# Layer norms of a hybrid convolution and attention kernel applied as one broadcast factor a token, with a second buffer for copied attention and an earlier norm of the next band

## The chip, the cores and the metric

The kernel runs on 1 core of one Trainium2 chip. The metric is the device time of one execution in microseconds (us). The kernel before took 956.23 us in the median of 9 runs (953.95 to 963.8).

## The reference, cut to what matters

The input x has 4 images of 128 channels on 64 x 64 pixels. Two layers follow each other.

```python
# layer 0: windowed attention
y = layernorm over channels (eps 1e-6) * g + b
y = y + depthwise 3x3 convolution(y)
# 16x16 windows, 2 branches, 4 heads of 32; each pixel attends to its 5x5 neighbours in the window
x = x + (ho[:, 0] + 0.5 * ho[:, 1]) / sqrt(1.25)

# layer 1: tokens t = pixels, 128 channels
t = t + linear_attention(ln(t), W, b)      # q, k = elu(.) + 1; causal sums over all earlier tokens
t = t + recurrence(ln(t), W, V)            # batch norm of ln(t) @ W.T, then y = sigmoid(wx + y @ V.T)

def ln(v, eps=1e-5):                       # over the 128 channels of a token
    return (v - mean(v)) / sqrt(var(v) + eps)
```

Both norms of layer 1 feed a matrix product over the channels. So (v - mean) @ W is v @ (C W) with C = I - 1/128, and the factor 1/sqrt(var + eps) of a token may be applied to the product's result as well as to its input.

## The kernel before, in words

The work is cut into 16 bands (4 images, 4 bands of 16 pixel rows each), a band into 4 windows of 16 x 16 pixels, and for layer 1 into 2 halves of 512 tokens. The order of the work is written by hand: one loop over 64 windows ("places") emits the instructions, and at its end `in_order` pins each of TensorE (PE), VectorE (DVE), ScalarE (ACT) and GpSimd (POOL) to the order of emission. The DMAs stand on SyncE's queue (SP) in the order of the framework's own scheduling. Every matmul result goes through one pool of 8 PSUM banks (`bank`, L172), taken in turn.

At place i three windows are in work, in this order:

- `logits` of window i (L362, L367), with exponentials on ACT (L376).
- `scaled` of window i - 2 on POOL (L425): the copied attention `o_sb` times the broadcast reciprocals `rden`, into `oT`.
- `weighted` of window i - 1: row sums (L385), their copy `den` (L388) and its DMA to `dc` (L390); weighted sums of values (L397) and their copy on ACT to `o_sb` (L405); reciprocals on DVE (L408 to L412), a DMA of them to DRAM (L414) and one from DRAM to all partitions, `rden` (L416). Both `o_sb` and `rden` have one buffer.
- `window_inputs` of window i + 1: queries, keys and values (L322 to L345).

Between these parts there are 6 numbered gaps a place (`between`, L678). In each gap two generators move on by one step:

- `behind` is layer 1 of the band before, `layer1` (L594), a written list of 24 steps of which 24 gaps of four places take one each, beginning at the second place of a band, gap 0. Its operations: `output0` (L450, L457: output projection and residual), `measure` (mean and variance by bn_stats on DVE, then 1/sqrt on POOL by L195, L196), `norm` (four DVE instructions of L203), `turn` (four PE transposes by L212, copied to SBUF by ACT, L474), `queries`, `keys`, `values` (L479 to L504), `scores`, `accumulate`, `attend`, and then, for the second norm, `measure` again, `norm`, `keep` (transposes of the un-normed tokens, an ACT copy, a DMA to DRAM), `turn_last` (transposes of the normed tokens, an ACT copy, L582) and `product` (L587, an ACT copy to `wx`, L588, statistics on DVE, L589).
- `ahead` is `front` (L648): layer norm of the next band (`norm_rows`, L212 with input `xf`) and its convolution (`convolve`, L271 and L273). In the first place of a band it moves only in gaps 0, 4 and 5. `norm_rows` measures group g, scales group g - 1 and turns group g - 2 in one step, so that a group's transposes come in the step after its scaling.

After the last place `run(behind)` and `layer1_end` finish layer 1 of the last band with nothing beside them. Then 8 MB of kept tokens come back by four DMAs (`res`, L733, two each on the SP and the ACT queue), and the recurrence runs: 11 warming steps and 32 steps of two groups (L756 to L808).

The lines that set the emission order of a gap:

```python
    def between(i, gap):
        next(behind, None)
        if i < len(places) and (i == 0 or i % NB or gap in (0, 4, 5)):
            next(ahead, None)
```

Of the kernel before, what the change touches and what calls it, by code (L numbers as in the profile page):

```python
# [46 lines left out]
def conv_attn_hybrid(ctx: ExitStack, tc: tile.TileContext, ins: dict, out: bass.AP):  # L47
# [10 lines left out]
    def loaded(name, shape, dt=F32, src=None, eng=None):  # L58
# [19 lines left out]
        pattern=[[1, P]],  # L78
        channel_multiplier=-1,
    )  # L80
    mhalf = const.tile([P, NCH], F32, name="mhalf")
    nc.vector.memset(mhalf, -0.5)

# [49 lines left out]
    def prepare():  # L133


        rect = math.sqrt(1.0 + LAM * LAM * (BR - 1))
        nc.vector.tensor_scalar(woT[:, 0], woT[:, 0], 1.0 / rect, None, ALU.mult)
        nc.vector.tensor_scalar(woT[:, 1], woT[:, 1], LAM / rect, None, ALU.mult)
        nc.vector.tensor_scalar(ab1, ab[:, :2], 1.0, None, ALU.add)


    dmax = const.tile([P, 16], F32, name="dmax")
# [56 lines left out]
    def normed(found, tiles, tag):  # L199
        pieces, mv, rs = found  # L200
        xn = tiles.tile([P, 4, P], F32, tag=tag, name=tag)
        for j, piece in enumerate(pieces):
            nc.vector.tensor_scalar(  # L203
                xn[:, j, :], piece, mv[:, j, 0:1], rs[:, j : j + 1], ALU.subtract, ALU.mult
            )
        return xn
# [17 lines left out]
    def norm_rows(n):  # L224

        b, wi = bands[n]
        y = padded(n)
        below = wi < NB - 1
        first, end = (0 if wi == 0 else 1), NCH + below

        def evict(dst, src):
            nc.scalar.activation(dst, src, AF.Identity, bias=ln_b, scale=ln_g)

        groups = [(0, 4), (4, 8), (8, 9)] if wi == 0 else [(1, 5), (5, end)]

        found, xn = {}, {}
        for g in range(len(groups) + 2):
            if g < len(groups):
                found[g] = measured(
                    [xin[n][:, j, :] if j < NCH else heads.pop(n + 1) for j in range(*groups[g])],  # L240
                    1e-6,
                )
            if g - 1 in found:
                xn[g - 1] = normed(found.pop(g - 1), p2, "xf")
            if g - 2 in xn:
                j0, j1 = groups[g - 2]
                rows = turned(xn.pop(g - 2), 0, j1 - j0)[:, : (j1 - j0) * P]
                rows = rows.rearrange("p (r w) -> p r w", w=W)
                k1 = min(2 * j1 + 1, WS + 2)
                evict(y[:, 2 * j0 + 1 : k1, 1 : W + 1], rows[:, : k1 - 2 * j0 - 1, :])  # L250
                if j1 > NCH:
                    evict(padded(n + 1)[:, 1:3, 1 : W + 1], rows[:, 2 * (NCH - j0) :, :])
            yield
        ks = slice(1, WS + 1 + below)
        nc.gpsimd.tensor_copy(y[:, ks, 0:1], y[:, ks, 1:2])
        nc.gpsimd.tensor_copy(y[:, ks, W + 1 :], y[:, ks, W : W + 1])

        if wi == 0:
            nc.gpsimd.tensor_copy(y[:, 0, :], y[:, 1, :])
        if below:  # L260
            nc.gpsimd.tensor_copy(padded(n + 1)[:, 0, :], y[:, WS, :])
        else:
            nc.gpsimd.tensor_copy(y[:, WS + 1, :], y[:, WS, :])
# [115 lines left out]
    def weighted(w):  # L379


        ops, dps = bank(), bank()
        for h in range(HEADS):
            rows = slice(h * HD, (h + 1) * HD)
            nc.tensor.matmul(dps[rows], ones[:, :HD], w["es", h], start=True, stop=True)  # L385

        den = p1.tile([P, BR * WT], F32, tag="den", name="den")
        nc.scalar.copy(den, dps)  # L388
        dc = p2.tile([P, 16], F32, tag="dc", name="dc")
        nc.sync.dma_start(dc, den[::HD, :])  # L390
# [13 lines left out]
        o_sb = p1.tile([P, BR * WT], F32, tag="o_sb", name="o_sb")  # L404
        nc.scalar.copy(o_sb, ops)  # L405
# [12 lines left out]
        yield  # L418
# [45 lines left out]
            del oTs[h.n], xin[h.n]  # L464

    def measure(h):
        h.found = measured([h.x[:, j, :] for j in range(4)], 1e-5)

    def norm(h):
        h.xn = normed(h.found, p3, "xn")  # L470

    def turn(h):
        h.xl = p2.tile([P, 512], F32, tag="xl", name="xl")
        nc.scalar.copy(h.xl, turned(h.xn, 0, 4))  # L474

    def feature(h, m):

# [95 lines left out]

    def keep(h):

        rs = p1.tile([P, SEG, HSEGS], F32, tag="rs_o", name="rs_o")
        nc.scalar.copy(rs, turned(h.x, 0, 4).rearrange("p (k s) -> p s k", s=SEG))
        nc.sync.dma_start(resd[h.b][:, h.hb], rs.rearrange("p s k -> p (s k)"))

    def turn_last(h):  # L580
        h.xl = p2.tile([P, 512], F32, tag="xl2", name="xl2")
        nc.scalar.copy(h.xl, turned(h.xn, 0, 4))  # L582

    def product(h):

        wps = bank()
        nc.tensor.matmul(wps, fwT, h.xl, start=True, stop=True)  # L587
        nc.scalar.copy(wx[:, h.b, h.hb], wps.rearrange("p (k s) -> p s k", s=SEG))  # L588
        nc.vector.bn_stats(  # L589
            stats[:, h.b * NH + h.hb, :], wx[:, h.b, h.hb].rearrange("p s k -> p (s k)")  # L590
        )

    def layer1(n, last):

        a, c = Half(n, 0), Half(n, 1)
        y, z = last
        order = [
            (keep, z), None,
            (norm, z), (product, y), None,
            (output0, a), (measure, a), None,  # L600
            (turn_last, z), None,
            (norm, a), (output0, c), (measure, c), None,
            (turn, a), None,
            (product, z), (norm, c), None,
            (queries, a), None,
            (keys, a), None,
            (turn, c), None,
            (values, a), None,
            (queries, c), None,
            (scores, a), None,  # L610
            (keys, c), None,
            (turn_keys, a), None,
            (values, c), None,
            (accumulate, a), None,
            (turn_keys, c), None,
            (attend, a, 0), None,
            (attend, a, 1), (measure, a), None,
            (scores, c), (keep, a), None,
            (accumulate, c), (norm, a), None,
            (attend, c, 0), None,  # L620
            (turn_last, a), (attend, c, 1), (measure, c), None,
        ]
# [7 lines left out]
    halves = {}  # L630

    def layer1_end(y, z):
        norm(z)
        product(y)
        yield
        keep(z)
        turn_last(z)
        yield
        product(z)

# [5 lines left out]
    def front():  # L646


        for n in range(1, len(bands)):
            yield from norm_rows(n)  # L650
            if bands[n][1]:
                yield
            for half in range(2):
                yield from convolve(n, half)
                yield
            if n == 1:

                for _ in range(4):
                    yield


    nc.vector.tensor_scalar(cpe_w[:, 4:5], cpe_w[:, 4:5], 1.0, None, ALU.add)
# [14 lines left out]
    def between(i, gap):  # L677


        next(behind, None)  # L680
        if i < len(places) and (i == 0 or i % NB or gap in (0, 4, 5)):
            next(ahead, None)

    for i in range(len(places) + 2):
# [5 lines left out]
        if 2 <= i:  # L690
            m, wjm = places[i - 2]
            if wjm == NB - 1:
                run(behind)
                behind = layer1(m, halves.pop(m - 1, (None, None)))
        between(i, 0)
        if 2 <= i:
            scaled(m, wjm, windows.pop(i - 2))
# [802 lines left out]
```

## Time and profile before

| what | value |
|---|---|
| median of 9 runs | 956.23 us |
| the profiled execution's own time | 954.84 us |
| its span, first to last instruction | 952.8 us |
| mean granted TensorE clock | 0.979 |
| PE busy | 877.9 us (92%) |
| DVE busy | 745.5 us (78%) |
| ACT busy | 543.5 us (57%) |
| POOL busy | 262.7 us (28%) |

Span and own time differ by 2.0 us, which lie around the first and the last instruction. A page line such as `L212 PE MATMUL bank<-ident,xn ... x256` is one group: source line, engine, operation, written and read tiles, count. In the views of waits, "A <- B: total, times, longest" says that A's engine was idle before A until B was done. In the view of windows each row is a stretch of time, then the busy time of PE, PEld (weight loads), DVE, ACT and POOL, the granted clock, the share of the 16 DMA engines that was busy and GB/s.

Of the span, about 33 us pass before the second place, the places and their gaps last until about 841 us, the end of layer 1 until 880 us, and the recurrence until 952.8 us.

### The profile page before, as it was taken

Reading aid. Unit: us, or ns where it says so; the run is one execution under the profiler, and the core shown is the slowest. Engines: PE = TensorE matmul, PEld = TensorE weight load, DVE = VectorE, ACT = ScalarE, POOL = GpSimd, SP = SyncE. Lnnn points to the kernel's source line nnn. Section 1 sums busy time; section 2 is a strip of 40 time slices with the busy share of each in tenths; the row PEclk is TensorE's granted clock in tenths of the full one; section 3 lists DMA queues with packets and bytes.
Section 4 is the critical chain, followed back from the end, with each engine's and each line's share of the span. In section 5 each row is a group of like instructions: output and inputs, shape, how many; then the busy total and the mean of one; then the engine's idle time right before and its main releaser. Section 6 shows DMA issues by size and latency. Waiting matters only on the chain.

```text
span 952.8 us, 26560 instructions
## 1 busy us (share of the span) xinstructions
PE 877.9 (92%) x10508; PEld 654.3 (69%) x10508; DVE 745.5 (78%) x2452; ACT 543.5 (57%) x1010; POOL 262.7 (28%) x359
## 2 busy tenths in 40 slices
PE   5979999999999999999999999999999999967784
PEld 3757777777777777677777777786767778645442
DVE  6445979887887878797878879887878787567786
ACT  3555656565756565665657565656666564522553
POOL 2113131413232322413132323223141312131185
PEclk9988999999999999999999999999999999999898
DMA  4111121211212121212112121211121111100853
GB/s 124 28 36 60 48 69 37 55 60 49 58 60 59 49 54 55 61 37 64 51 47 59 58 58 58 51 58 55 48 69 36 55 39 51 40 34 30 352 205 148
DMA packets 53045, 63.46 MB, mean 67 GB/s; under 512 B 22960, under 2 KB 33840, under 8 KB 52400
## 3 DMA queue, kind: packets, MB, share of 16 engines
q1 hardware_dynamic: 51184, 56.91, 19.1%
q10 hardware_dynamic: 1728, 4.77, 1.3%
q8 instruction: 85, 1.39, 0.6%
q14 instruction: 48, 0.39, 0.1%
HBM read 35.44 MB, written 17.30 MB: 55 GB/s over the span
## 4 chain that ended last, share of the span: by engine, by line
PE 69%; DMA 10%; DVE 9%; ACT 5%; POOL 3%; issue 2%; SPq 1%; ACTq 0%; POOLq 0%; DVEq 0%
PE bank L322 9%; PE bank L450 6%; PE bank L367 6%; PE bank L212 6%; DMA rden<-rd 6%; PE bank L397 5%; PE bank L385 5%; PE bank L335 5%; PE bank L479 5%; PE bank L558 3%; PE bank L587 3%; PE bank L539 3%; PE bank L522 3%; PE bank L560 3%; DMA res<-resd 2%
## 5 line engine op out<-in xcount | busy, mean ns | idle before, releaser
L273 DVE SCALAR_TENSOR_TENSOR y<-ypad,cpe_w,y 128x512 f32<-128x512 f32 x240 | 188.7, 786 | 12.9 <-ACT y L271 9.3
L425 POOL TENSOR_TENSOR oT<-o_sb,rden 128x512 f32<-128x512 f32 x64 | 85.3, 1332 | 361.2 <-DMA rden<-rd 335.0
L376 ACT ACTIVATE es<-bank 128x512 f32<-128x512 f32 x256 | 132.2, 602 | 77.2 <-PE bank L367 77.2
L196 POOL TENSOR_TENSOR rs<-rs,mhalf 128x4 f32<-128x4 f32 (+2 forms) x100 | 106.8, 1068 | 8.3
L367 PEld LDWEIGHTS bank<-q,k 32*128 32x128 f32 x3072 | 99.0, 191 | 10.7 <-ACT k L330 9.6
L367 PE MATMUL bank<-q,k 32*128 32x96 f32 (+1 forms) x3072 | 97.6, 273 | 8.7 <-ACT k L330 8.7
L203 DVE TENSOR_SCALAR xn<-x,mv,rs 128x128 f32<-128x128 f32 x256 | 83.3, 386 | 21.5 <-POOL rs L196 21.5
L195 POOL TENSOR_SCALAR rs<-mv 128x4 f32<-128x4 f32 (+2 forms) x100 | 24.9, 249 | 269.6 <-DVE mv L193 181.8
L397 PEld LDWEIGHTS bank<-es,v_sb 128*32 128x32 f32 x3072 | 57.2, 111 | 30.5 <-issue 18.7
L405 ACT COPY o_sb<-bank 128x512 f32<-128x512 f32 x64 | 37.6, 587 | 66.5 <-POOL oT L425 48.3
L479 PE MATMUL bank<-xl,awT 128*128 128x512 f32 x128 | 70.1, 631 | 1.0 <-ACT xl L474 1.0
L385 PE MATMUL bank<-es,ones 128*32 128x512 f32 x512 | 70.8, 626 | 0.0
L397 PE MATMUL bank<-es,v_sb 128*32 128x96 f32 (+1 forms) x3072 | 70.3, 240 | 0.0
L450 PE MATMUL bank<-woT,oT 128*128 128x128 f32 x512 | 65.6, 283 | 4.1 <-POOL oT L425 4.0
L450 PEld LDWEIGHTS bank<-woT,oT 128*128 128x128 f32 x512 | 62.4, 196 | 7.9 <-POOL oT L425 5.1
L322 PE MATMUL bank<-y2w,wqT 128*128 128x256 f32 x256 | 66.3, 382 | 1.4 <-DVE y2w L273 1.4
L342 ACT COPY v_sb<-bank 128x512 f32<-128x512 f32 x64 | 37.6, 588 | 51.3 <-PE bank L335 50.3
L322 PE MATMUL bank<-y2w,wkT 128*128 128x256 f32 x256 | 65.8, 380 | 0.0
L335 PE MATMUL bank<-wvT,y2w 128*128 128x256 f32 x256 | 65.8, 380 | 0.0
L330 ACT COPY q<-bank 128x512 f32<-128x512 f32 x64 | 37.8, 591 | 37.8 <-PE bank L322 37.4
L191 DVE BATCH_NORM_STATS2 st<-x 128x6 f32<-128x128 f32 x256 | 55.5, 279 | 1.1
L212 PE MATMUL bank<-ident,xf 128*128 128x128 f32 x128 | 31.5, 332 | 24.5 <-DVE xf L203 20.4
(124 smaller groups left out, 1741.7 us busy)
## 6 DMA issues: line engine op xcount, KB each, us to landing
rden<-rd SPq DMA_DIRECT2D x64, 256.0 KB
v_sb<-v_sb SPq DMA_DIRECT2D x128, 64.0 KB
resd<-rs_o SPq DMA_DIRECT2D x32, 256.0 KB
out<-ot SPq DMA_DIRECT2D x32, 256.0 KB
xin<-in_xt SPq DMA_DIRECT2D x15, 512.0 KB
res<-resd SPq DMA_DIRECT2D x2, 2048.0 KB
res<-resd ACTq DMA_DIRECT2D x2, 2048.0 KB
dc<-den SPq DMA_DIRECT2D x64, 8.0 KB
```

Source lines behind the costliest of these rows:

```text
L196: nc.gpsimd.tensor_tensor(rs[:, :n], rs[:, :n], mhalf[:, :n], ALU.pow)
L212: nc.tensor.transpose(tps[:, j * P : (j + 1) * P], xn[:, j0 + j, :], ident)
L273: nc.vector.scalar_tensor_tensor(y2, src, cpe_w[:, tap : tap + 1], y2, ALU.mult, ALU.add)
L322: nc.tensor.matmul(pps[:, br * WT : (br + 1) * WT], wT[:, br * P : (br + 1) * P], y2, start=True, stop=True,)
L335: nc.tensor.matmul(vps[:, e * 256 : (e + 1) * 256], y2[:, e * P : (e + 1) * P], wvT, start=True, stop=True,)
L367: nc.tensor.matmul(sps[h][:, cols], w["k"][rows, k0 : k0 + P], w["q"][rows, cols], start=False, stop=(br, n) == pieces[-1],)
L376: nc.scalar.activation(es, sps[h], AF.Exp, scale=scale)
L385: nc.tensor.matmul(dps[rows], ones[:, :HD], w["es", h], start=True, stop=True)
L397: nc.tensor.matmul(ops[rows, cols], w["v"][:, n, c0 : c0 + HD], w["es", h][:, cols], start=(br, n) == pieces[0], stop=(br, n) == pieces[-1],)
L425: nc.gpsimd.tensor_tensor(oTs[n][:, :, :, wj * WS : (wj + 1) * WS], w["o"].rearrange("p (a r c) -> p a r c", a=BR, c=WS), w["rden"].rearra ...
L450: nc.tensor.matmul(yps[:, j * P : (j + 1) * P], oT[:, br, t], woT[:, br, :], start=br == 0, stop=br == BR - 1,)
L479: nc.tensor.matmul(zps, awT[:, m * P : (m + 1) * P], h.xl, start=True, stop=True)
```

## The change

It has three parts.

1. `o_sb` is taken from the pool of two buffers in place of the one of one.
2. `norm_rows` is cut into separate steps (measure, measure, scale, then turn, scale and measure of successive groups). In a band's first place `ahead` moves in gaps 0, 2 and 4, so that measuring begins in the first gap and goes on in every second one; `convolve` loses one yield, and the pause after band 1 is 3 steps and lies between the halves.
3. Layer 1's norms: `norm` and `turn_last` are gone. The channel mean is taken out of the weights once (`centre` multiplies `awT` and `fwT` by I - 1/128). `measure` sends its 128 x 4 factors to DRAM by one DMA and back to all partitions by a second (`rs_b`, 128 x 512); both stand on SP. `turn` multiplies the transposed tokens in PSUM by the factors on DVE, where ACT copied them. `product` takes the tokens that `keep` transposed, and DVE multiplies its result by the factors on the way to `wx`, where ACT copied it. The list of steps is spread anew: the second `output0` comes one step sooner (step 4), `turn` of the first half moves from step 6 to 7, its `queries` from 8 to 9, together with `turn` of the second half.

```diff
+    center = const.tile([P, P], F32, name="center")
+    nc.vector.tensor_scalar(center, ident, -1.0 / P, None, ALU.add)
...
+    def centre(w):
+
+        cps = bank()[:, : w.shape[1]]
+        nc.tensor.matmul(cps, center, w, start=True, stop=True)
+        nc.vector.tensor_copy(w, cps)
...
-        for g in range(len(groups) + 2):
-            if g < len(groups):
-                found[g] = measured(
...
-            if g - 1 in found:
-                xn[g - 1] = normed(found.pop(g - 1), p2, "xf")
-            if g - 2 in xn:
...
+        measure(0)
+        yield
+        measure(1)
+        yield
+        scale(0)
+        yield
+        for g in range(len(groups)):
+            turn(g)
+            scale(g + 1)
+            measure(g + 2)
             yield
...
-        o_sb = p1.tile([P, BR * WT], F32, tag="o_sb", name="o_sb")
+        o_sb = p2.tile([P, BR * WT], F32, tag="o_sb", name="o_sb")
...
     def measure(h):
-        h.found = measured([h.x[:, j, :] for j in range(4)], 1e-5)
-
-    def norm(h):
-        h.xn = normed(h.found, p3, "xn")
+
+        _, _, rs = measured([h.x[:, j, :] for j in range(4)], 1e-5)
+        there = dram4.tile([P, 4], F32, tag="rs_d", name="rs_d")
+        nc.sync.dma_start(there, rs)
+        h.rs = p3.tile([P, 512], F32, tag="rs_b", name="rs_b")
+        nc.sync.dma_start(h.rs, there.rearrange("p j -> (p j)").partition_broadcast(P))
 
     def turn(h):
         h.xl = p2.tile([P, 512], F32, tag="xl", name="xl")
-        nc.scalar.copy(h.xl, turned(h.xn, 0, 4))
+        nc.vector.tensor_tensor(
+            h.xl.rearrange("p (j t) -> p j t", j=4),
+            turned(h.x, 0, 4).rearrange("p (j t) -> p j t", j=4),
+            h.rs.rearrange("p (t j) -> p j t", j=4),
+            ALU.mult,
+        )
...
-        rs = p1.tile([P, SEG, HSEGS], F32, tag="rs_o", name="rs_o")
-        nc.scalar.copy(rs, turned(h.x, 0, 4).rearrange("p (k s) -> p s k", s=SEG))
-        nc.sync.dma_start(resd[h.b][:, h.hb], rs.rearrange("p s k -> p (s k)"))
-
-    def turn_last(h):
-        h.xl = p2.tile([P, 512], F32, tag="xl2", name="xl2")
-        nc.scalar.copy(h.xl, turned(h.xn, 0, 4))
+        h.xs = p2.tile([P, SEG, HSEGS], F32, tag="rs_o", name="rs_o")
+        nc.scalar.copy(h.xs, turned(h.x, 0, 4).rearrange("p (k s) -> p s k", s=SEG))
+        nc.sync.dma_start(resd[h.b][:, h.hb], h.xs.rearrange("p s k -> p (s k)"))
 
     def product(h):
 
         wps = bank()
-        nc.tensor.matmul(wps, fwT, h.xl, start=True, stop=True)
-        nc.scalar.copy(wx[:, h.b, h.hb], wps.rearrange("p (k s) -> p s k", s=SEG))
+        nc.tensor.matmul(wps, fwT, h.xs.rearrange("p s k -> p (s k)"), start=True, stop=True)
+        n = P // SEG
+        nc.vector.tensor_tensor(
+            wx[:, h.b, h.hb].rearrange("p s (j n) -> p s j n", n=n),
+            wps.rearrange("p (s j n) -> p s j n", n=n, j=4),
+            h.rs.rearrange("p (n s j) -> p s j n", n=n, j=4),
+            ALU.mult,
+        )
...
-            (norm, z), (product, y), None,
+            (product, y), None,
             (output0, a), (measure, a), None,
-            (turn_last, z), None,
-            (norm, a), (output0, c), (measure, c), None,
+            (output0, c), (measure, c), None,
+            None,
+            (product, z), None,
             (turn, a), None,
-            (product, z), (norm, c), None,
-            (queries, a), None,
+            None,
+            (queries, a), (turn, c), None,
             (keys, a), None,
-            (turn, c), None,
...
     def layer1_end(y, z):
-        norm(z)
         product(y)
         yield
         keep(z)
-        turn_last(z)
         yield
         product(z)
...
-        if i < len(places) and (i == 0 or i % NB or gap in (0, 4, 5)):
+        if i < len(places) and (i == 0 or i % NB or gap in (0, 2, 4)):
             next(ahead, None)
...
+        if i == 2:
+            centre(awT)
+            centre(fwT)
```

More of the change, by code (lines that the diff above doesn't have):

```diff
@@ L236, in norm_rows, with measure, scale, turn @@
         found, xn = {}, {}
-        for g in range(len(groups) + 2):
+        def measure(g):
             if g < len(groups):
-                found[g] = measured(
-                    [xin[n][:, j, :] if j < NCH else heads.pop(n + 1) for j in range(*groups[g])],
-                    1e-6,
-                )
-            if g - 1 in found:
-                xn[g - 1] = normed(found.pop(g - 1), p2, "xf")
-            if g - 2 in xn:
[L246 to L252, printed above, removed]
+                pieces = [
+                    xin[n][:, j, :] if j < NCH else heads.pop(n + 1) for j in range(*groups[g])
+                ]
+                found[g] = measured(pieces, 1e-6)
+        def scale(g):
+            if g < len(groups):
+                xn[g] = normed(found.pop(g), p2, "xf")
+        def turn(g):
+            j0, j1 = groups[g]
+            rows = turned(xn.pop(g), 0, j1 - j0)[:, : (j1 - j0) * P]
+            rows = rows.rearrange("p (r w) -> p r w", w=W)
+            k1 = min(2 * j1 + 1, WS + 2)
+            evict(y[:, 2 * j0 + 1 : k1, 1 : W + 1], rows[:, : k1 - 2 * j0 - 1, :])
+            if j1 > NCH:
+                evict(padded(n + 1)[:, 1:3, 1 : W + 1], rows[:, 2 * (NCH - j0) :, :])
+        measure(0)
[8 more added lines that the diff above has]
+            measure(g + 2)
             yield
@@ L618, in layer1 @@
             (scores, c), (keep, a), None,
-            (accumulate, c), (norm, a), None,
+            (accumulate, c), None,
             (attend, c, 0), None,
-            (turn_last, a), (attend, c, 1), (measure, c), None,
+            (attend, c, 1), (measure, c), None,
         ]
@@ L652, in front @@
                 yield
-            for half in range(2):
-                yield from convolve(n, half)
-                yield
+            yield from convolve(n, 0)
+            yield
             if n == 1:
-                for _ in range(4):
+                for _ in range(3):
                     yield
+            yield from convolve(n, 1)
     nc.vector.tensor_scalar(cpe_w[:, 4:5], cpe_w[:, 4:5], 1.0, None, ALU.add)
```

## The prediction, as it was put on record

> **What bounds the kernel now.** I began with the view of windows, one row for a stretch of steady bands and one for the start.
>
> ```profile
> 238.00:357.00 119.00, 115.99 (x1495) 87.34 (x1495) 99.31 (x320) 73.66 (x132) 31.98 (x45) 1.00 0.20 56
> ...
> 45.00:55.00 10.00, 4.94 (x64) 3.40 (x66) 5.78 (x10) 4.29 (x9) 1.26 (x1) 0.75 0.11 28
> ```
>
> In the steady part PE is busy 115.99 of 119 us and DVE, next, 99.31: PE's order is the bound, so a saving counts if it takes work or a wait from PE. In the start PE is busy 4.94 of 10 us, at clock 0.75: something else sets the pace. So I read the waits of PE from 119 to 833 us, and then all waits from 24 to 119 us.
>
> ```profile
> PE bank L212 <- DVE xf L203: 11.6, 9, 1.3
> PE bank L212 <- ACT es L376: 4.1, 4, 1.0
> PE bank L539 <- ACT k L516: 3.5, 5, 0.8
> ```
>
> ```profile
> POOL oT L425 <- DMA rden<-rd: 54.9, 6, 14.1
> ACT o_sb L405 <- POOL oT L425: 16.6, 6, 4.6
> ...
> PE bank L367 <- ACT k L330: 8.7, 3, 5.1
> ```
>
> Of PE's 19.2 us of recorded waits in the steady part, 15.7 stand at the transposes of `norm_rows` (I take the second line for the same wait: its xf tile was written just before). In the start PE waits for a key copy (5.1 us at once), ACT's copies stand behind `o_sb`, and `o_sb` waits for POOL, which waits for `rden`. The chain of work shows that loop and its period, and below it two later pieces that I use.
>
> ```profile
> 46.94 1.27 POOL oT L425
> ...
> 52.78 4.83 DMA rden<-rd
> 57.74 1.28 POOL oT L425
> ...
> 67.75 1.27 POOL oT L425
> ...
> 354.69 2.19 DMA rd<-rc
> ...
> 880.59 22.78 DMA res<-resd
> ```
>
> Three periods from 46.94 to 77.31 us, 10.1 us each, of which DMA and POOL are only 6.1. Last, PE's timeline in one band, for the price of transposes, and two windows for the DMAs:
>
> ```profile
> 331.54 1.00 PE L212 MATMUL bank<-ident,xf 128*128 128x128 f32 x4 [1.03 <-ACT es L376]
> ...
> 338.89 0.60 PE L212 MATMUL bank<-ident,xn 128*128 128x128 f32 x4
> 339.33 1.03 PE L322 MATMUL bank<-y2w,wkT 128*128 128x256 f32 x4
> ```
>
> ```profile
> 358.40:361.00 2.60, 2.60 (x56) 1.40 (x53) 1.09 (x3) 2.50 (x5) 0.00 (x0) 1.00 0.26 97
> ...
> 376.10:376.80 0.70, 0.70 (x6) 0.65 (x5) 0.56 (x3) 0.00 (x0) 0.00 (x0) 1.00 0.99 356
> ```
>
> Four transposes cost 0.44 us from start to the next start. The first DMA window is one `rden` (issued at 356.96), the second one a kept half (issued at 375.23): both move 128 rows of 2 KB, one with a quarter of the engines in 2.6 us, one with all in 0.7.
>
> [...]
>
> **The change, part by part.** The sum is made against the profiled execution, 954.84 us, which is 1.4 us below the median of 956.23.
>
> *Transposes.* `turn_last` goes: 32 halves x 0.44 = 14.1 us off PE, all on the path but the last two or three.
>
> *Norm of the band ahead.* Scaling of the first group now stands in gap 4 of the place before its transposes, so the xf wait should go: 15.7 us. The transposes that do run also trail DVE: 0.94 us from start to start at 331.54, against 0.44. I count 0.3 us in 14 bands, 4 us, for that (0 to 7). Moved with it, POOL's 1/sqrt (1.3 us) stands ahead of a `scaled` that waits for `rden` anyway.
>
> *Copied attention.* With two `o_sb`, ACT needn't wait for POOL, but `rden` keeps its one buffer, so a period still holds DMA 4.8, POOL 1.3 and about 0.2 of issue: 6.3 us. Three periods at 6.3 in place of 10.1 give 11.4 us; PE's work of that stretch is below that (busy 24.8 us from 45 to 78.65, part of it at clock 0.75). I take 10 (5 to 11.4). In the steady part ACT's 27.5 us of this wait hold no PE wait; nothing is counted.
>
> *ACT and DVE.* ACT loses 96 copies of about 0.6 us, 57 us. DVE loses 256 scalings (83.3 us busy) and gains 64 multiplications of 0.69 (44 us[...]). Neither is the bound: nothing, as long as DVE, 83% busy in the steady part, stays below PE. `centre`: two matmuls and two copies, about 1.1 us of PE in the start, inside PE's slack there.
>
> *The round trip, steady.* This is the new wait. `turn` waits on DVE for `rs_b`; behind it queue the convolution, `queries`' evictions and the reciprocals; PE waits at `queries` of the first half. From the end of `output0` to that matmul PE has, by start-to-start times of this band: queries 0.86, second output 1.78, keys 0.87, values 0.87, product 1.05, logits 1.64, transposes 0.44, row sums 1.00, weighted sums 1.02: 9.5 us. Against it: 338.03 to 341.48 for addition, statistics and POOL, 3.45; issue 0.1; the DMA to DRAM, like `rd`, 1.5 to 2.2, say 1.6 (L414 issued 340.48, L416 follows at 341.93); the broadcast, `rden`'s 4.74 less the 2.0 that 16 engines save, 2.7; DVE 0.7 and hand-overs 0.25. That is 8.8. But in SP's order the next band's `xin` (512 KB) now stands ahead of it, and that transfer fills all engines for about 2 us (share 1.00 from 344.70 to 346.50): up to 1.3 more, 10.1. I take a wait of 0.6 us a band, 14 bands, 8.4 us; bounds 0 and 1.4 (0 and 20 us). The other round trips have 6 steps, about 13 us, and are covered.
>
> SP also carries 128 more DMAs of 0.3 to 0.6 us, each first one waiting for POOL and each second one for the first: `rd` and `rden` behind them come about 1 us later. Cover: `oT` was done 1.9 us before `output0` began (334.22 to 336.14), and 1 us of it is left. Without it PE would pay what is over.
>
> *The end.* With nothing beside it, the round trip is bare. First: `queries` began 5.7 us after `output0` ended (848.8 to 854.46), now about 9.3; the second half's follow closer, and at the last `measure` 2 us remain. Last: in SP's order the 2 MB `res` of image 0 stands ahead of the last `rs_b`, because it waits only for the last product's matmul. 8 MB took 22.8 us, so the two 2 MB copies at the heads of both rings take 11.4[...]. Against `wx` ready at 880.5 this is about 894 (879 + 1.3 + 11.4 + 1.2 + 0.7 = 893.6), 13 to 14 us later. The recurrence had 2 to 3 us of that to spare (it waited for `res` until 903.46). I take 12.5 us; bounds 4 (the broadcast isn't held) and 15.
>
> Sum: -14.1 - 15.7 - 4 - 10 + 8.4 + 12.5 = -22.9. The profiled execution would take 932, a median 933.
>
> **The rivals.**
> *The last broadcast is not held.* If rings let it pass, the end costs 4 in place of 12.5: 925. For: 256 KB is small[...].
> *Waits move, not vanish.* If the xf wait only turns into another one of DVE's (convolution before the scaling) and the start is held by `rden`, what is left is -14.1 - 5 + 8.4 + 12.5 = +1.8: 958. For: DVE is 83% busy; against: PE waits for little else than xf.
> *The round trip sets the band (slower).* Place: the DVE multiplication of `turn`. If the broadcast takes what `rden` takes beside `xin` (341.93 to 347.92, 6.0 us) and the DMA before it 2.2, the wait is 3.45 + 0.1 + 2.2 + 6.0 + 0.95 - 9.5 = 3.2 us a band, 45 us: -43.8 + 45 + 12.5 = +13.7, 970. It decides from 2.2 us a band (31.3 us). For: 128 reads of one row of DRAM, not seen at this size[...].
>
> **How the numbers follow.** Forecast 0.66 (921 to 944, from the bounds of the wait, the start and the end); end not held 0.20 (916 to 927); waits move 0.07; round trip sets the band 0.07. The range from 917 to 945 leaves out the last two and the tails. About 0.3% (2.9 us) is what a measurement of this kernel can tell from no change. Faster: 0.66 + 0.20 + 0.02 of the third; same 0.05 of it; slower 0.07.
>
> **What would show it.** The xf waits gone from PE's list; the first `oT`s 6 to 7 us apart; L474 (the new `output0`) first begun near 68 us; a wait of PE for `xl` at `queries` below 1.4 us a band; `rs_b` landing about 2.7 us after issue at a high DMA share; the last `wx` near 13 us after the last product. I am wrong if PE waits over 2 us a band for `xl`, if bands aren't about 1.8 us shorter than the 51.7 that lies between the first outputs of two bands (284.44 to 336.14), or if the end costs what a band saves.

## The result, and the profile after

The changed kernel took 1032.44 us in the median of 10 runs (1027.47 to 1037.38), the kernel before 957.75 in 31. The ratio is 1.078, 95% interval 1.076 to 1.080. The forecast was 933 with a range of 917 to 945, so it had the wrong sign, by 99 us.

I cut each profiled execution into three: the start (up to the first matmul of `output0`), the bands (from there to the first matmul of the last band's `output0`), and the end. Line numbers are each kernel's own; in the changed kernel `output0` is L474, `oT` is L449, `queries` is L510.

| profiled execution | span | start | bands | end |
|---|---|---|---|---|
| before | 952.8 | 78.7 | 766.6 | 107.5 |
| changed | 1030.4 | 76.9 | 824.1 | 129.4 |
| predicted difference | -22.9 | -10 | -25 | +12.5 |
| measured difference | +77.6 | -1.7 | +57.5 | +21.9 |

The window of steady bands comes first: stretch, its length, busy time of PE, PEld, DVE, ACT and POOL, granted clock, DMA share, GB/s.

```profile
238.00:357.00 119.00, 106.81 (x1363) 82.29 (x1362) 90.40 (x295) 60.18 (x110) 29.36 (x43) 0.99 0.28 72
```

PE fell from 115.99 to 106.81 busy and DVE from 99.31 to 90.40. No engine took PE's place: all have become idler, and the bound is a wait. PE's waits from 119 to 900 us, and four lines of SP's own waits over the whole span:

```profile
PE bank L474 <- POOL oT L449: 33.3, 14, 3.3
PE bank L510 <- DVE xl L500: 28.1, 19, 2.6
```

```profile
SPq L496 <- DMA rs_d<-rs: 128.1, 47, 5.5
SPq L494 <- POOL ypad L280: 64.1, 14, 11.1
SPq L494 <- POOL rs L204: 60.8, 15, 4.5
SPq L494 <- POOL rs L205: 48.1, 25, 7.4
```

The xf waits are gone, as forecast. Of the new ones two are large: one for `xl`, which the prediction had named, and one for `oT`, the older loop of `rd` and `rden`, which it had called covered. SP spends 128 us standing at the broadcast (L496) until the copy before it has landed. It also stands at that first copy, `rs_d` (L494), until POOL has the factors (the other three lines, 173 us in all). In the chain of work of one band, start and duration of each piece:

```profile
350.85 3.56 DMA rd<-rc
354.43 5.02 DMA rden<-rd
359.49 0.09 issue
359.58 1.27 POOL oT L449
360.85 0.04 issue
360.89 2.05 PE bank L474 x16
...
370.53 6.11 DMA rs_d<-rs
376.65 3.13 DMA rs_b<-rs_d
```

`rd` takes 3.56 us where the line shown of before had 2.19, and PE begins `output0` the moment `oT` is there. `rs_d`, 2 KB, takes 6.11 us where I had put 1.6. With only the 8 KB `dc` beside it, `rs_b` takes 3.13 against my 2.7. While it moves, from 377.8 to 379.4 us, the DMA share is 0.45 to 0.53: that is above the 0.26 of `rden`'s window in the prediction, but about half of the full share (0.99) that the kept half reached there. That `rs_b` would use all engines was my supposition, and these windows don't bear it out. Start and end show two more pieces, the second with SP's timeline:

```profile
52.38 4.88 DMA dc<-den
...
939.01 17.59 DMA rs_b<-rs_d
956.63 1.03 DVE wx L616
```

```profile
938.64 0.32 SPq L767 DMA_DIRECT2D res<-resd  x1
939.01 0.43 SPq L496 DMA_DIRECT2D rs_b<-rs_d  x1
```

In the start the 8 KB copy `dc`, issued 0.7 us after an `rden`, takes 4.88 us. At the end the last broadcast, issued 0.37 us after a `res` of 2 MB, takes 17.6 us; that it would be late there was forecast.

### The profile page after: what moved, and what is told of

Same layout as the page of the kernel before. It is cut to its first block, busy times and chain, and to the rows that moved or that the text cites. A ratio compares the mean times of both kernels' runs of the same rounds, so it can differ in the third digit from the quotient of the medians.

```text
span 1030.4 us, 26158 instructions
## 1 busy us (share of the span) xinstructions
PE 874.9 (85%) x10384; PEld 661.8 (64%) x10384; DVE 730.7 (71%) x2263; ACT 489.2 (47%) x914; POOL 251.8 (24%) x359
## 3 DMA queue, kind: packets, MB, share of 16 engines
q1 hardware_dynamic: 69616, 73.83, 25.7%
q10 hardware_dynamic: 1728, 4.77, 1.2%
## 4 chain that ended last, share of the span: by engine, by line
DVE 32%; DMA 29%; PE 27%; POOL 4%; issue 3%; ACT 3%; SPq 0%; ACTq 0%; DVEq 0%; POOLq 0%
DVE y L297 10%; DMA rden<-rd 8%; DMA rs_b<-rs_d 7%; PE bank L474 7%; DMA rs_d<-rs 6%; DMA rd<-rc 5%; PE bank L346 4%; DVE st L200 4%; PE bank L510 3%; DVE state L578 3%; DVE f L515 2%; POOL oT L449 2%; PE bank L391 2%; DVE x L603 2%; DVE low L514 2%
## 5 line engine op out<-in xcount | busy, mean ns | idle before, releaser
L297 DVE SCALAR_TENSOR_TENSOR y<-ypad,cpe_w,y 128x512 f32<-128x512 f32 x240 | 183.1, 763 | 26.7 <-ACT y L295 22.7
L449 POOL TENSOR_TENSOR oT<-o_sb,rden 128x512 f32<-128x512 f32 x64 | 83.5, 1304 | 361.2 <-DMA rden<-rd 244.2
L474 PE MATMUL bank<-woT,oT 128*128 128x128 f32 x512 | 75.6, 310 | 43.9 <-POOL oT L449 43.9
L510 PE MATMUL bank<-xl,awT 128*128 128x512 f32 x128 | 73.0, 654 | 39.4 <-DVE xl L500 38.3
L474 PEld LDWEIGHTS bank<-woT,oT 128*128 128x128 f32 x512 | 72.3, 222 | 48.9 <-POOL oT L449 47.9
L205 POOL TENSOR_TENSOR rs<-rs,mhalf 128x4 f32<-128x4 f32 (+2 forms) x100 | 99.0, 990 | 8.3
L481 DVE TENSOR_TENSOR x<-bank,xin 128x512 f32<-128x512 f32 x32 | 22.1, 691 | 89.4 <-PE bank L474 89.4
L512 ACT ACTIVATE low<-bank,ab 128x512 f32<-128x512 f32 x64 | 44.0, 688 | 81.8 <-PE bank L510 81.5
L500 DVE TENSOR_TENSOR xl<-bank,rs_b 128x512 f32<-128x512 f32 x32 | 34.1, 1065 | 55.4 <-DMA rs_b<-rs_d 51.8
L346 PE MATMUL bank<-y2w,wqT 128*128 128x256 f32 x256 | 71.9, 406 | 1.0 <-DVE y2w L297 1.0
L514 DVE TENSOR_SCALAR low<-low 128x512 f32<-128x512 f32 x64 | 39.7, 620 | 36.3 <-ACT low L512 36.3
L616 DVE TENSOR_TENSOR wx<-bank,rs_b 128x512 f32<-128x512 f32 x32 | 33.9, 1060 | 40.7 <-DMA rs_b<-rs_d 21.6
```

The source lines that it names most:

```text
L205: nc.gpsimd.tensor_tensor(rs[:, :n], rs[:, :n], mhalf[:, :n], ALU.pow)
L297: nc.vector.scalar_tensor_tensor(y2, src, cpe_w[:, tap : tap + 1], y2, ALU.mult, ALU.add)
L346: nc.tensor.matmul(pps[:, br * WT : (br + 1) * WT], wT[:, br * P : (br + 1) * P], y2, start=True, stop=True,)
L449: nc.gpsimd.tensor_tensor(oTs[n][:, :, :, wj * WS : (wj + 1) * WS], w["o"].rearrange("p (a r c) -> p a r c", a=BR, c=WS), w["rden"].rearra ...
L474: nc.tensor.matmul(yps[:, j * P : (j + 1) * P], oT[:, br, t], woT[:, br, :], start=br == 0, stop=br == BR - 1,)
L510: nc.tensor.matmul(zps, awT[:, m * P : (m + 1) * P], h.xl, start=True, stop=True)
```

## The experiments

Times are medians; the kernel before, timed again beside each group, gave 955.9 to 960.9, so across groups the ratios are compared. "Ring theory" is what I held first: the new DMAs on SP's one queue and in its ring delay the older ones. By a ring I mean the copies that one engine issues: the page of the changed kernel counts 73.83 MB in one queue (q1) and 4.77 MB, which by their sizes are ACT's, in another (q10). That one ring's copies pass in the order of issue was my assumption. I split it later into a wait theory and a load theory.

**The parts one by one.** Part 1 alone is one word (`o_sb` from `p2`), part 2 alone is `norm_rows`, `front` and `between`, and the third kernel has both. Part 3 alone is all the rest.

> The kernel before with a second o_sb buffer alone (part 1). Ring theory (the loss of the whole change comes from the new DMAs on SP's one queue and ring): this part is harmless; with the o_sb wait gone, dc stands behind rden in SP's ring, as the start of the changed kernel shows (oT at 48.41, 57.22, 65.93, 75.63, periods of 8.7 to 9.7 us), so the start shrinks by about 1 us a period, 3 to 5 us: 953 to 955. The prediction's own step says 10 us less, 947. Rival (parts 1 and 2 give nothing or cost): 957 or more.

> The kernel before with the new order of norm_rows and front alone (part 2). Ring theory: the xf waits of PE go and nothing takes their place, 15.7 to 20 us less: 938 to 942. Rival (the waits only move to another DVE instruction): 950 to 958.

> The kernel before with parts 1 and 2, layer 1's norms as they were. Ring theory: the two gains add, 20 to 25 us less than before, 932 to 938, and the whole loss of the change is part 3's. Rival (parts 1 and 2 are part of the loss): 950 or more.

> Part 3 alone: layer 1's norms as one factor a token by two DMAs, with one o_sb and the old norm_rows. Ring theory: it loses what the change lost and the gain of the other parts besides, about 75 + 20: 1040 to 1060. The prediction's sum without parts 1 and 2 says -14.1 + 8.4 + 12.5, 964. Rival (parts 1 and 2 are part of the loss): below 1020.

| kernel | time | ratio to before (95%) | start | bands | end |
|---|---|---|---|---|---|
| part 1 | 943.71 | 0.983 (0.979 to 0.987) | 73.5 | 759.7 | 109.5 |
| part 2 | 938.33 | 0.978 (0.974 to 0.982) | 78.6 | 746.3 | 112.6 |
| parts 1 and 2 | 932.75 | 0.973 (0.969 to 0.977) | 78.4 | 744.3 | 106.9 |
| part 3 | 1026.09 | 1.068 (1.063 to 1.073) | 79.4 | 818.1 | 127.7 |

Parts 1 and 2 are gains without part 3, so the rival that put the main loss on them is out. They don't add by the medians: 15.5 and 20.9 us alone, 26.5 together. Part 3 alone loses 67 us, less than I had expected. With the other two parts the loss is 75, and the intervals of the ratios (1.063 to 1.073, and 1.076 to 1.080) don't touch: beside part 3 the other parts gain nothing and cost about 1%, most of it in the bands (818.1 and 824.1). Why is not shown.

**The round trip taken apart.** In three kernels the two multiplications take a tile of ones, so that nothing reads the broadcast.

```diff
+    const_rs = const.tile([P, 512], F32, name="const_rs")
+    nc.vector.memset(const_rs, 1.0)
...
-            h.rs.rearrange("p (t j) -> p j t", j=4),
+            const_rs.rearrange("p (t j) -> p j t", j=4),
```

The first still sends and broadcasts the factors; the second leaves `rs_d` and `rs_b` out; the third is the second with a view of unit step, `"p (j t) -> p j t"`.

> The changed kernel, with both multiplications taking their factors from a tile of ones read by the same stepped view; the factors are still sent to DRAM and broadcast, and nothing reads them. Leaves out the division by the standard deviation in layer 1. Ring theory (the new copies and SP's waits for them also hold up rd and rden): the wait of PE for xl goes, its wait for oT of 2.7 us a band stays, so about half of the loss stays: 960 to 990. Rival A (only the wait for rs_b in DVE's order costs): 915 to 930. Rival B (DVE's own work is the loss): above 1000.

> The changed kernel without rs_d and rs_b: the multiplications take a tile of ones by the same stepped view. Leaves out the division by the standard deviation in layer 1. Ring theory and rival A: parts 1 and 2 gave 26.5 us, the 128 transposes left out give 14 more, and nothing is paid: 915 to 922. Rival B (DVE's stepped multiplications and its order are the loss): 980 or more.

> As the one without round trips, with the tile of ones read by unit steps in both multiplications. Leaves out the division by the standard deviation in layer 1. Ring theory and rival A: each multiplication falls from 1.05 to about 0.7 us, 64 of them, 22 us of DVE's time, and the kernel's time stays within 4 us of the stepped one. Rival B: 15 us or more faster than the stepped one.

Measured: 1001.93 (ratio 1.050, 1.044 to 1.055), 920.19 (0.963, 0.958 to 0.968) and 915.44 (0.958, 0.953 to 0.962). This decides most. With all of DVE's and PE's new work but without the trips the kernel is 37 us faster than before, so DVE's work is not the loss; with unit steps a multiplication takes 0.69 us in place of 1.06, and the kernel gains about 5 us, which the intervals hardly tell from nothing. Trips that nobody reads cost 82 us, more than I had expected; waiting for their result costs about 30 more. By stage (no trip: 76.8, 735.8, 106.2; trips unread: 74.9, 813.5, 108.9):

- trips that nobody reads: +77.7 us in the bands, +2.7 at the end;
- the wait for their result: +10.6 in the bands, +20.5 at the end.

Three rows of windows for the bands, of the kernel without trips, the one with unread trips, and the changed one:

```profile
77.00:812.00 735.00, 717.09 (x9329) 555.56 (x9328) 609.32 (x1914) 409.35 (x738) 197.08 (x283) 0.99 0.18 56
```

```profile
75.00:888.00 813.00, 740.97 (x9329) 572.59 (x9329) 610.27 (x1914) 408.14 (x738) 194.86 (x283) 0.97 0.26 70
```

```profile
77.00:901.00 824.00, 737.53 (x9329) 569.34 (x9329) 609.16 (x1914) 408.63 (x738) 196.22 (x283) 0.97 0.26 69
```

Same instructions on PE, and PE idle for 17.9, 72.0 and 86.5 us. Besides, its busy time grew by 24 us with the unread trips, at a lower mean clock (0.97 for 0.99): it is lower after some of the waits, down to 0.50 (see the last section). SP's timeline of the kernel with unread trips shows how a copy that nobody reads holds others up:

```profile
364.26 0.32 SPq L497 DMA_DIRECT2D rs_d<-rs  x1
364.68 0.51 SPq L368 DMA_DIRECT2D v_sb<-v_sb  x1
365.24 0.63 SPq L369 DMA_DIRECT2D v_sb<-v_sb  x1
370.53 0.33 SPq L499 DMA_DIRECT2D rs_b<-rs_d  x1
370.89 0.58 SPq L414 DMA_DIRECT2D dc<-den  x1
```

ACT had copied `den` by 367.3 us. `dc` is issued at 370.89, 3.6 us later, because SP stood at `rs_b` until `rs_d`, 6.3 us on its way, had landed. DVE waits for `dc` in order (34.5 us in this run, 5.6 without trips), and its later work stands behind that wait. At the end of the band comes the second place, here for three bands (us in each trace):

| kernel | reciprocals ready | `rd` issued | `rden` issued | `oT` begun | `output0` begun | PE's wait for it |
|---|---|---|---|---|---|---|
| no trip | 366.21 | 366.24 | 368.09 | 373.76 | 375.12 | 0 |
| trips unread | 397.06 | 398.53 | 401.52 | 406.61 | 407.96 | 2.11 |
| changed | 349.54 | 350.85 | 354.43 | 359.58 | 360.89 | 2.42 |

From the reciprocals to `rden`'s issue it is 1.9, 4.5 and 4.9 us. Here SP doesn't stand at `rs_b`. It stands at `rs_d` until POOL has the factors (at 397.13 us with unread trips; `rs_d` is issued at 397.15), a kept half (`resd`) goes next, and `rd` is issued 1.5 us after the reciprocals (1.3 in the changed kernel). Then `rd` itself takes longer: 3.0 and 3.6 us to `rden`'s issue, against 1.85. Over 13 bands that stretch has a median of 3.2 us in both kernels with trips and of 1.9 without.

**Waiting or load.** One kernel keeps SP's waits and drops the 256 KB. The other keeps the 256 KB and drops `rs_d`, with the wait for POOL and for its flight.

```diff
-        h.rs = p3.tile([P, 512], F32, tag="rs_b", name="rs_b")
-        nc.sync.dma_start(h.rs, there.rearrange("p j -> (p j)").partition_broadcast(P))
+        h.rs = p3.tile([P, 4], F32, tag="rs_b", name="rs_b")
+        nc.sync.dma_start(h.rs, there)
```

```diff
-        there = dram4.tile([P, 4], F32, tag="rs_d", name="rs_d")
-        nc.sync.dma_start(there, rs)
         h.rs = p3.tile([P, 512], F32, tag="rs_b", name="rs_b")
+        nc.vector.memset(h.rs[:1, :1], 0.0)
         nc.sync.dma_start(h.rs, there.rearrange("p j -> (p j)").partition_broadcast(P))
```

> The changed kernel with a tile of ones as factors, as in the run where nothing reads the broadcast, but rs_d comes back as 128 x 4 (2 KB) in place of the 256 KB broadcast. Leaves out the division by the standard deviation in layer 1. The loss to be split is the 82 us between 920.2 (no trip at all) and 1001.9 (trips that nobody reads). Wait theory (SP stands at the second copy until rs_d has landed, and dc, rd and rden stand behind it): most of the 82 us stays, 970 to 1002. Load theory (256 KB ahead of rden, rd and dc in the ring): 920 to 940.

> As the run where nothing reads the broadcast, but rs_d is written once at the start, and each of the 64 broadcasts of 256 KB reads that same row, after a one-element memset on DVE at its old place: the load on the ring stays, the wait for rs_d goes. Leaves out the division by the standard deviation in layer 1. Wait theory: 920 to 945. Load theory: 970 to 1002.

Measured: 975.15 (1.016, 1.010 to 1.022) and 953.43 (0.995, 0.992 to 0.998). Above the trip-free 920.19 that is 55 and 33 us, and their sum, 88, is near the 82 of both. The second one's runs spread from 942 to 956, and its profiled execution was at the low edge, so its 33 is uncertain by several us. The bands, first with the waits kept, then with the load kept:

```profile
75.00:867.00 792.00, 740.17 (x9330) 577.79 (x9331) 602.27 (x1914) 411.26 (x738) 197.86 (x284) 0.96 0.20 52
```

```profile
75.00:832.00 757.00, 718.71 (x9329) 559.46 (x9329) 609.50 (x1974) 409.05 (x738) 196.79 (x284) 0.99 0.26 75
```

| kernel | PE busy in the bands | PE idle in the bands | PE's wait for `oT`, whole run | DVE's wait for `dc`, whole run |
|---|---|---|---|---|
| no trip | 717.1 | 17.9 | 6.4 | 5.6 |
| load kept | 718.7 | 38.3 | 31.6 | 5.9 |
| waits kept | 740.2 | 51.8 | 42.9 | 9.9 |
| trips unread | 741.0 | 72.0 | 42.9 | 34.5 |

So the waits alone bring the whole wait for `oT` and nearly all of PE's longer busy time. With the 256 KB added, DVE's wait for `dc` grows from 9.9 to 34.5 us and PE's idle time by another 20. The waits are the larger part, but the split isn't clean. The first kernel keeps the issue of 128 copies and SP's wait for POOL. In the second SP still stands at the broadcast, now for the memset in DVE's order (93.6 and 47.5 us in two lines of its waits), so its 33 us are not load alone.

**Other queues.** If SP's standing is the cost, POOL or ACT might issue the pair (`nc.gpsimd` or `nc.scalar` for `nc.sync` in both lines). I tried POOL on the full change and on a smaller version of it: parts 1 and 2, with the factor by DMA for the second norm only, whose result is needed six steps later.

> Parts 1 and 2, and the factor by DMA for the second norm only (product); the first norm is scaled on DVE as in the kernel before. Ring theory: the trip of product has six steps of cover, so bands lose only what rd and rden are delayed by half as many copies (0 to 1.4 us a band), gain 14 us of transposes, and the end pays 14 to 20 us for the last broadcast behind res: 935 to 955 against 932.75 for parts 1 and 2. Rival A: bands gain the 14 us in full, 932 to 939. Rival B: above 960.

> The changed kernel in full, with rs_d and rs_b issued by POOL, so that SP has neither the copies nor the wait. Wait theory: rd, rden and dc come as early as without trips; what stays is PE's wait for xl and POOL's own stand at rs_b: 940 to 975. Load theory: the same 256 KB still share the engines with rden, 990 or more.

> Parts 1 and 2 and the factor by DMA for the second norm only (960.9 on SP's queue), with rs_d and rs_b issued by POOL. Wait theory: the 42 us that the trips cost on SP go in large part: 922 to 940. Load theory: 950 to 961.

Measured: 960.89 for the smaller version on SP (1.004, 1.001 to 1.006), that is 41 us above its trip-free level, for which I take the 920 of the kernel without trips as an estimate (no trip-free version of the smaller kernel was run): half the trips, half of the 82. POOL made it far worse: 1115.78 in full, 1005.13 for the smaller one. My expectation missed the same wait in a new place. POOL's timeline of the full version, with its idle time before each instruction in brackets:

```profile
381.15 0.61 POOL L494 DMA_DIRECT2D rs_d<-rs  x1 [0.29 <-POOL rs L205]
384.36 0.54 POOL L496 DMA_DIRECT2D rs_b<-rs_d  x1 [2.60 <-DMA rs_d<-rs]
384.91 1.27 POOL L449 TENSOR_TENSOR oT<-o_sb,rden 128x512 f32<-128x512 f32 x1
```

The wait now stands ahead of `oT` itself, which PE was short of already: over the run POOL stands 141.0 us at `rs_b`, and PE's wait for `oT` is 68.0 us, against 43.9 in the changed kernel. That isn't all. POOL's padding copies for the convolution (`ypad`) are late too: ACT waits 101.7 us for them, against 35.8. How the loss divides between the two I did not test.

**Issued later.** Next, the smaller version with `rs_d` emitted one step after its factors and `rs_b` two or three steps later, on SP and on ACT; the full change in the same way on ACT; and the changed kernel with only the last band's pair on ACT.

```diff
-            (scores, c), (keep, a), None,
+            (scores, c), (keep, a), (send, a), None,
...
-            (attend, c, 0), None,
+            (attend, c, 0), (spread, a), None,
```

> Parts 1 and 2 and the factor by DMA for the second norm only (960.9), with rs_d issued one step after its factors and rs_b two or three steps after rs_d, both still on SP. Wait theory: SP no longer stands, so two thirds of the 42 us that these trips cost go, and the ring load of 32 broadcasts stays: 928 to 940. Load theory: 950 or more.

> The same with both copies on ACT's queue, so in the other ring. If the load costs by its place ahead of dc, rd and rden in SP's ring: 5 to 15 us less than with the copies on SP, 918 to 932. If it costs because the same 16 engines carry it: within 4 us of the copies on SP. If ACT stands at them: above 945.

> The whole change with both copies on ACT's queue, rs_d a step after its factors and rs_b a step or two after that. Wait theory: the bands lose only PE's wait for xl, which has one step less of cover than in the changed kernel (up to 3 us a band), and the end its bare trip: 930 to 970. Rival (the trip of the first norm cannot be covered in any queue): 985 or more.

> The changed kernel, with rs_d and rs_b of the last band alone on ACT's queue, so that the last broadcast no longer stands behind the 2 MB res in SP's ring. Ring theory: DVE's 16.9 us wait for rs_b at the last product falls to about 5, and the end gives back 10 to 16 us: 1014 to 1024. Rival (the 2 MB copies on the engines delay it in any ring): 1028 to 1034.

*On SP*: 965.11 (1.006, 1.003 to 1.009), no better. The edit hardly reached the queue: SP isn't pinned to the emission order, and its timeline still has the pair around `rd`. Over the run it stands 55.1 us at `rs_b` for `rs_d`, as before the edit (55.4).

```profile
387.15 0.32 SPq L498 DMA_DIRECT2D rs_d<-rs  x1
387.52 0.63 SPq L613 DMA_DIRECT2D resd<-rs_o  x1
388.27 0.36 SPq L438 DMA_DIRECT2D rd<-rc  x1
388.89 0.32 SPq L502 DMA_DIRECT2D rs_b<-rs_d  x1
391.31 0.58 SPq L440 DMA_DIRECT2D rden<-rd  x1
```

So this run says nothing on the wait theory. *On ACT*: 954.54 (0.998, 0.995 to 1.000), still 34 us above the trip-free level with SP free of both copies. That is in the range that I had given for ACT standing at them, and ACT does stand 2.50 us at `rs_d` in the band that I read, 32.4 us over the run. The chain of work of this band doesn't go through that, though; it and ACT's timeline show what PE waits for:

```profile
374.85 1.69 DMA rd<-rc
...
376.61 8.20 DMA rden<-rd
```

```profile
376.78 0.33 ACTq L502 DMA_DIRECT2D rs_b<-rs_d  x1
```

`rd` is short again, but `rden`, 5 us elsewhere, takes 8.20, with a broadcast issued 0.17 us after it in the other ring: about the 3.1 us of an `rs_b` longer. It isn't this band alone: over 13 bands the last `rden` took 7.8 us in the median from its issue to the start of `oT`, against 5.5 in the changed kernel. So the loss doesn't need a place in SP's ring: `rden` is long here with the broadcast in ACT's. How the two rings' copies share the engines is not shown.

*The full change on ACT*: 1046.03, worse than on SP; the rival was right. DVE waits 57.5 us for `rs_b` there, PE 23.6 for `xl` and 35.5 for `oT`. *The end*: 1023.03 (1.069, 1.064 to 1.073), in the ring theory's range: the last `rs_b` is issued at 940.52 us, 4.6 us ahead of ACT's `res` (945.16), the longest wait of DVE at the last product falls from 16.9 to 3.0 us, and the end from 129.4 to 117.3. What ends last then is `res` itself (23.11 us in the chain). As `rs_b` no longer moves beside `res`, this run doesn't tell whether its place in the ring or the load of `res` had held it.

**The broadcast moved out of the way.** Same copies on ACT, but the first half's broadcast waits for the next `output0`, and both products follow later.

```diff
-            (output0, a), (measure, a), (spread, z), None,
-            None,
+            (output0, a), (measure, a), (spread, y), None,
+            (spread, z), None,
...
-            (attend, c, 0), (spread, a), None,
+            (attend, c, 0), None,
```

> As the run with both late copies on ACT's queue (954.5), but the broadcast of a band's first half is held back to the step of the next output0, when the last rden has landed and the next is not yet issued, and the second half's to the step after; the two products follow three and four steps later. Place theory (the broadcast costs only where it meets the last rden of a band): the 36 us go, 919 to 930, below the 932.75 of parts 1 and 2. Load theory (256 KB more cost wherever they stand): 945 to 958.

Measured: 944.02 (0.983, 0.979 to 0.986). Of the 34 us, 10.5 came back (1.5% of the time before, 14 us, by the ratios), so place counts, but the run is just below the load theory's range and far above the place theory's. Its bands take 745.9 us, as long as those of parts 1 and 2 with the transposes (744.3), and PE still waits 28.3 us for `oT`, the last `rden` taking 5.8 us in the band that I read. The bands alone gave back 18.6 us of the 764.5 of the run before it. Its end is 119.1 against 110.6 there, after an edit that moved both products of the last band back too. What else holds its bands I did not find out.

**A small copy moved.** Parts 1 and 2, with `nc.scalar.dma_start(dc, ...)`.

> Parts 1 and 2 (932.75), with the copy dc<-den issued by ACT in place of SP. Ring theory: dc lands about 1.9 us after its issue in the start also, the first four oT come 6 to 7.5 us apart in place of 8.4 to 9.9, the first output begins 3 to 8 us sooner, and bands stay: 924 to 931. Rival (the shared engines delay dc in any ring, or ACT's issue costs as much): 931 to 938.

Measured: 940.84 (0.984, 0.981 to 0.987), slower than with `dc` on SP. Beside `rden`, `dc` took 4.00 us in ACT's ring (4.60 in SP's), the first output began at 77.35 in place of 78.39 us, and the bands grew from 744.3 to 751.7. The ring theory fell for this copy as well; why the bands grew is not shown. Of all kernels that do the whole computation, parts 1 and 2 alone are the fastest, 932.75 us.

## Why the prediction was wrong, step by step

- *The step that failed*: "`rd` and `rden` behind them come about 1 us later", with "1 us of it is left". I priced 128 DMAs by their time on SP's queue, 0.3 to 0.6 us, and not by what they hold up. The step was entered as nothing, and trips that nobody reads cost 77.7 us in the bands, 5.2 a band. SP stands at `rs_d` until POOL has the factors (173 us in three lines of its waits), and at 47 of the 64 `rs_b` until `rs_d` has landed (128.1 us); `dc`, `rd` and `rden` stand behind. The 256 KB are under way beside them as well. I had found both waits ("each first one waiting for POOL and each second one for the first") but gave them no length. The second one's length is `rs_d`'s flight, which I took as 1.6 us from a free `rd`; the chain of the changed kernel has 6.11. At PE's wait for `oT` the delay was 2.6 to 3.0 us in the bands of the table, not 1.
- *Its cover*: I measured 1.9 us at one place. The delay enters at two, and by way of `dc` it reaches DVE's order. Without cover, I wrote, "PE would pay what is over"; in fact it paid more: its busy time grew by 24 us besides, at a lower clock (0.97 for 0.99).
- *The round trip at `queries`*: the place was right; PE arrived 9.5 us after `output0`, as worked out (362.78 to 372.29). The size was not: it waited 2.57 us in the band that I read and 28.1 us from 119 to 900 us, about 2 us a band where I had 0.6, and `rs_d`'s 6.11 us for 1.6 is the term that was off. That reading the result adds only 10.6 us to the bands, near my 8.4, is luck: it comes on top of bands that the unread trips had already stretched.
- *Transposes, xf wait and trailing transposes*: right. Part 2 gave 20.9 us for 19.7. For the 128 transposes, 14.1, the nearest measure is the kernel without trips: 12.6 us faster than parts 1 and 2 by the medians, 9 by the ratios. It differs in DVE's and ACT's work too, so the term isn't measured alone.
- *Copied attention*: 10 us predicted for the start; part 1 alone gave 5.1 there, and 6.9 in the bands, where "nothing is counted". The loop of 6.3 us left out `dc`, which takes 4.88 us when issued 0.7 us after an `rden`: four `oT`s at 48.41, 57.22, 65.93 and 75.63 us in the changed kernel, 8.7 to 9.7 apart. I did not test what the 6.9 are.
- *DVE*: rightly nothing. My 0.69 us was near an addition of the same size in the trace of before (0.684 us at L457). The stepped operand did cost, 1.06 us for 0.69, and is worth about 5 us, hardly clear of the noise.
- *The end*: the place was right (the last broadcast, issued just after a `res`), the term was too small: 12.6 us from issue to landing (11.4 behind the 2 MB copies, 1.2 for itself), 17.59 measured. That it would pass only after those copies was my estimate, and the runs don't show it. In all I had 12.5 us, and 21.9 were measured; 12.1 of them came back when the last band's pair left SP's queue.
- *The rival* that ended slower had the right sign but the wrong place: it put 45 us on PE's wait for `xl`, where 10.6 came, and no rival named `oT`.

## What to carry to other kernels

In this kernel a DMA that waited for another DMA held up what stood behind it on the engine that issued it (128.1 us on SP over the run; 2.60 us ahead of one `oT` on POOL, where POOL issued the pair), whether or not its result was urgent. Before adding such a pair, list what stands behind it in program order and who waits for that, and price the wait by a flight beside traffic (6.11 us for `rs_d`), not by a free one (my 1.6). Changing the queue moved the wait and didn't remove it, and with the broadcast in another queue `rden` took 8.20 us in the band that I read, for 5 elsewhere. A DMA round trip of 256 KB to save four transposes of 0.44 us together was a bad trade here, where a loop of DMAs had only 1 to 2 us of cover.

## What the runs showed of the hardware

Some waits of PE were followed by a lower clock. In the kernel with unread trips PE idled for 1.89 us ahead of 354.16; the windows after it (clock is the third number from the right) are

```profile
354.00:355.00 1.00, 0.84 (x7) 0.84 (x8) 0.00 (x0) 0.00 (x0) 0.11 (x1) 1.00 0.01 2
355.00:356.00 1.00, 1.00 (x8) 1.00 (x8) 0.00 (x0) 0.00 (x0) 0.00 (x0) 0.62 0.46 184
356.00:357.00 1.00, 1.00 (x6) 1.00 (x6) 0.00 (x0) 0.00 (x0) 0.00 (x0) 0.50 0.89 324
357.00:358.00 1.00, 1.00 (x3) 0.80 (x3) 0.94 (x3) 0.00 (x0) 0.00 (x0) 0.50 0.08 22
358.00:359.00 1.00, 1.00 (x6) 0.84 (x5) 0.97 (x10) 0.26 (x1) 0.00 (x1) 0.68 0.00 0
359.00:360.00 1.00, 1.00 (x11) 1.00 (x10) 0.36 (x3) 0.32 (x1) 0.92 (x2) 1.00 0.00 0
```

From some 1 us after PE had resumed, the clock is 0.62, 0.50, 0.50 and 0.68 in four windows, in which PE is busy throughout; then it is 1.00 again. A wait of 2.11 us before 407.96 was followed by clock 1.00. In the changed kernel, read in windows of 1 us from 119 to 900 us, the clock falls to 0.50 in ten stretches, and in each case one of the four windows before the first low one has no PE work in it; but its wait of 2.42 us before 360.89 was followed by 1.00. What decides is not shown. Over the bands of the kernel with unread trips PE's busy time is 24 us longer than without trips, beside 54 us of added idling.

The other surprise is how long some small copies took beside large ones: `rs_d`, 2 KB, issued 1.0 us after an `rden` of 256 KB, 6.11 us in the chain; and `dc`, 8 KB, 4.60 us (parts 1 and 2) and 4.88 us (changed) soon after an `rden` in SP's ring, and 4.00 beside one in ACT's. In the start of before `dc` took 1.88 us, at 37.30, with the DMA share at 0.04.
